# A hybrid attention, state-space and binary-weight kernel: statistics on another engine, identity products at the start, other table and product slots in the scan

## The chip, the cores and the metric

The kernel runs on one core of one Trainium2 chip. The metric is device time in microseconds (us) of one launch, the median of several runs. The core's engines work side by side, each through its own queue in order: TensorE (PE in the profile, its weight loads PEld), VectorE (DVE), ScalarE (ACT), GpSimd (POOL) and SyncE (SP), which here only issues DMAs. An instruction that has to wait holds up everything behind it on its engine.

## The reference

`x` is 4 batches of 1024 rows of 128 channels, float32. Four blocks follow one another, each with a residual sum and a layer norm ahead of it: windowed and strided attention with 16 heads of 8, a three-layer perceptron (MLP) with weights +1 and -1, a selective state-space block (256 inner channels, 16 states), and the MLP again.

```python
x = x + attention(layernorm(x), Wq, Wk, Wv, Wo)
x = x + mlp(layernorm(x), k0, k1, k2, s0, s1, s2)
x = x + mamba(layernorm(x), ln_g, ln_b, W_in, conv_w, ...)   # has its own residual inside
x = x + mlp(layernorm(x), k0, k1, k2, s0, s1, s2)
...
# the recurrence in mamba, for each of 256 channels and 16 states
dA = jnp.exp(dt_t[..., None] * A)
h = dA * h + (dt_t * u_t)[..., None] * B_t[:, None, :]
y_t = jnp.einsum('ben,bn->be', h, C_t)
```

## The kernel before

**Layout.** The batches go in two pairs. `xs[0]` and `xs[1]` hold a pair each: 128 partitions are 64 rows of each of the two batches, and 16 tiles `m` of 128 channels lie along the free dimension. A chunk `c` is 4 such tiles.

**Attention** (line 199) loops over 32 tiles, 16 of each pair, as a pipeline written out by hand: step `i` does the scores of tile `i+1`, the softmax of tile `i`, the strided products of tile `i-1` on GpSimd, their sums on VectorE, and so on to the residual of tile `i-5`. All its instructions are recorded while `keep` holds a value, so each engine runs them in the order in which they are written. The setup computes the first layer norm statistics and turns the weights: `weights_in` (line 232) transposes four weights on TensorE as soon as they are loaded. The residual of a tile `m` under 8 is a VectorE sum, that of a later tile a ScalarE copy from PSUM (`residual`, line 552). For pair 0 the statistics of the MLP behind the attention are taken in the loop too (`mlp_stats`).

**The stage between** (the `while` at line 1390) runs the first pair's MLPs and what the first scan needs. Here `keep` is empty, and a scheduler is free to place the instructions on each engine's queue, also among those of the attention ahead of them.

**The scans** (line 1097) are 128 units: 8 parts (a batch and a half of its 1024 steps; the order is `parts_in_order`), with 16 states `n` each. A unit `i` is:

- GpSimd: `drive(i)` makes `db`, the product of `du` with a row of B (128x1024);
- ScalarE: `decay(i, h)`, for each of the halves `h` of the 256 channels, makes `da = exp(dt * A)` (128x512);
- VectorE: two scans (128x512, `tensor_tensor_scan`) and, for most units, two products with the row of C into `hc`. For the states in `BY_GP` GpSimd makes this product instead, one 128x1024 instruction (`product_by_gp`); the scan then writes to `hs` and not over `da`;
- TensorE: turns `hc` with the identity and sums it over the states in PSUM.

`da` has three buffers in all and `db` three, so a decay can start only when the scan or product that last read its buffer is done. In a part that is the first half of its batch, ScalarE also copies the last column of each half's scan (`carry`).

**The planner.** The rest of the work (the MLPs of both pairs, the norms, what later parts need) is cut into pieces and put between the units by `pieces` (line 1328), by estimated costs of the engines. In each unit it is called twice: once between `decay(i+1, 0)` and `decay(i+1, 1)`, once behind both and behind the sums. A piece that empties PSUM banks is an eviction; one marked `lump` is a *table visit*: two ScalarE activations (Silu for `gate` and `u`, Softplus for `dt`) that need another function table than the exponential of the decays, so a table load stands ahead of them and another behind. A visit may come only where `pieces` is called with `lumps` true. Order on each engine is then kept as recorded.

**Statistics of the MLP behind pair 1's attention** (`stats_ahead(("a", 1, c), ...)`, line 1406) are a stream of such pieces in the scans. `ln_sums` (line 148) takes them there on ScalarE: for each tile an Identity and a Square activation with a sum, and each of these has an accumulator read behind it; four small GpSimd instructions of `ln_stats` and two scalings follow for each chunk. With `soon=True` it takes them on VectorE (`bn_stats`, `bn_aggr`) and needs no scaling.

**The tail.** Behind the last unit the remaining MLP pieces run, then the MLP of the last half.

The core of the loop over the units, from line 1240 on:

```python
product_by_gp(i - 1)
drive(i + 2)
decay(i + 1, 0)
...            # the scans and the VectorE products of unit i
pieces(t + 1.3)
...            # carry copies around decay(i + 1, 1), kept sums
pieces(t + 2.2, lumps=False)
```

Of the kernel before, what the change touches and what calls it, by code (L numbers as in the profile page):

```python
# [26 lines left out]
P = 128  # L27
# [10 lines left out]
E, N, DC, DR = 256, 16, 4, 8  # L38
# [5 lines left out]
def hybrid_kernel(ctx: ExitStack, tc: tile.TileContext, x, Wq, Wk, Wv, Wo, ln_g, ln_b, W_in, conv_w,  # L44
# [17 lines left out]
    ve, te, sc, gp = (InOrder(e) for e in (nc.vector, nc.tensor, nc.scalar, nc.gpsimd))  # L62
# [18 lines left out]
    xs = []  # L81
    for bp in range(NP):
        t = xpool.tile([P, NT, C], F32, tag=f"x{bp}", name=f"x{bp}")
# [11 lines left out]
    ident = const.tile([P, P], F32, name="ident")  # L95
# [103 lines left out]
    def attention(actx):  # L199
# [11 lines left out]
        def spare(name):  # L211
            return pr.tile([P, CH], F32, tag="pr", name=name)
# [16 lines left out]
        load_x(0, range(1, NT // 4), nc.sync)  # L229
        load_x(1, range(NT // 4), nc.sync)  # L230

        def weights_in():
            wt = spare("wt")
            for i in range(4):
                te.transpose(wt[:, i * C : (i + 1) * C], wsrc[:, i], ident)
            sc.copy(wqkv.rearrange("p i c -> p (i c)"), wt[:, : 3 * C])
            sc.copy(woT, wt[:, 3 * C :])


        norms, sums = {}, {}  # L240
# [347 lines left out]
        last = len(tiles)  # L588
# [140 lines left out]
    CT = NT // 4  # L729
# [92 lines left out]
    def stats_ahead(key, needs, tiles_of, soon=False):  # L822
        yield Piece(ready=lambda: all(k in fed for k in needs), same=True)
        known[key] = yield from ln_stats(tiles_of(), "f" + "_".join(map(str, key)), soon)
# [78 lines left out]
    units = [(b, f, n) for b, f in parts_in_order for n in range(N)]  # L903
# [193 lines left out]
    def scans(wide, ready):  # L1097
# [2 lines left out]

        bss, css, dbs, das, hss, hs_of = {}, {}, {}, {}, {}, {}
        BY_GP = (4, 6, 9, 11, 14)
        DIRECT = 1
        sums, kept, py, turned = {}, {}, {}, []
        last = len(units) - 1
# [20 lines left out]
                )  # L1126

        def by_gp(i):
            return units[i][2] in BY_GP and i < last - 1

        def product_by_gp(i):

# [100 lines left out]
        for i, (b, f, n) in enumerate(units):  # L1233
            now[0] = i
            load(i + 3)
            product_by_gp(i - 1)
            drive(i + 2)
            done["db", i + 2] = spend("gp", 2.38, *after(("hs", i - 1, 1)))
            decay(i + 1, 0)
            done["da", i + 1, 0] = spend("sc", 0.69, *after(("hc", i - 1)))  # L1240
            db = dbs.pop(i)
            hss[i] = m2.tile([P, NH, CH], F32, name=f"hc{i}", tag="hc", bufs=5)
            if by_gp(i):
                hs = hs_of[i] = m1.tile([P, NH, CH], F32, name=f"hs{i}", tag="hs", bufs=2)
                hs = [hs[:, h] for h in range(NH)]
            else:
                hs = [das[i, h] for h in range(NH)]
            for h in range(NH):
                first = carry[b % 2][:, h, n : n + 1] if f else 0.0
                ve.tensor_tensor_scan(hs[h], das.pop((i, h)), db[:, h], first, ALU.mult, ALU.add)  # L1250
                done["hs", i, h] = spend("ve", 1.2 if f else 1.14, *after(("da", i, h), ("db", i)))
            if not by_gp(i):
                for h in range(NH):
                    ve.tensor_mul(hss[i][:, h], hs[h], row_of(css, i))
                    done["half", i, h] = spend("ve", 0.6)
                done["hc", i] = times["ve"]
            t = times["ve"]
            pieces(t + 1.3)
            for h in range(NH):
                if f == 0:  # L1260
                    sc.copy(carry[b % 2][:, h, n : n + 1], hs[h][:, CH - 1 :])
                    spend("sc", 0.17, *after(("hs", i, h), ("half", i, h)))
                if h == 0:
                    decay(i + 1, 1)
                    done["da", i + 1, 1] = spend("sc", 0.67, *after(("hs", i, 0), ("half", i, 0)))
            for part in over(i, 1):
                keep_sum(*part)
                done["kept", i] = spend("sc", 0.6, *after(("sum", i - 1)))
            done["sum", i] = spend("pe", total(i), *after(("kept", i)))
            for part in over(i, 0) if i == last else ():  # L1270
                keep_sum(*part)
                turn_sum(*part)
                spend("pe", 0.5, spend("sc", 0.6, times["pe"]))
            t = times["ve"]
            pieces(t + 2.2, lumps=False)
        total(last + 1)
        for h in range(NH):
            gate_by(*units[last][:2], h)
# [3 lines left out]
    times = dict(pe=0.0, ve=0.0, sc=0.0, gp=0.0)  # L1282
# [45 lines left out]
    def pieces(until, lumps=True):  # L1328

        forced = not until
        evictions(lumps, forced)
        for k, rate in RATES.items():
            owed[k] = min(max(owed[k], -2 * rate) + (0 if forced else rate / 2), rate / 2)
        left = SPARE - sum(w.held for w in works)

        for w in works[:-2] + sorted(works[-2:], key=lambda w: w.count):

            moved = w in emptied and now[0] < len(units) - 10  # L1340
            while w.may() and not w.next.evict and w.next.banks <= left:
                if moved and not w.next.same and not (forced and w in emptied):
                    break
                if not (forced or w.next.hurries()):
                    if any(us and owed[k] <= 0 for k, us in w.next.us.items()):
                        break
                    if "pe" in w.next.us and ends(w)[0]["pe"] > until:
                        break
                left -= w.next.banks
                issue(w)  # L1350
                moved = True
            if forced and moved:
                break
# [5 lines left out]
    def stream(*kinds):  # L1359
        for k in kinds:  # L1360
            yield from k
# [5 lines left out]
    def in_scan_buffers(u):  # L1367
# [5 lines left out]
    lanes = [  # L1373
        Work(stream(
            early(0, lane, f1, lane, *[in_scan_buffers] * lane),
            early(0, 2 + lane, f1, lane),
            early(1, lane, f1, lane),
            early(1, 2 + lane, f1, lane),
            *(late(0, 2 * q + lane, f1, lane) for q in range(CT // 2)),
            late_batch(B - 2 + lane, 0, range(4), f1, lane),  # L1380
            late_batch(B - 2, 1, range(2 * lane, 2 * lane + 2), f1, lane),
# [3 lines left out]
    with banks(8):  # L1385
        first = [
            Work(stream(*(mamba_norm(0, c) for c in first_half))),
            Work(mamba_pre_half(*parts_in_order[0])),
        ]
        while (*parts_in_order[0], NH - 1) not in prepared:  # L1390
            wanted = first[-1].may() and "pe" in first[-1].next.us
            for w in first + ([] if wanted else lanes):
                if w.may():
                    w.run()
        for w in lanes:
            while w.next.evict or w.held:
                w.run()
    with banks(SPARE), tc.tile_pool(name="wide", bufs=1, space=PSUM) as wide:
        keep.append(True)
        works.extend([  # L1400
            first[-1],
            Work(stream(*(mamba_pre_half(*k) for k in parts_in_order[1:]))),
            Work(stream(*(mamba_norm(0, c) for c in second_half), *(mamba_norm(1, c) for c in range(CT)))),
            Work(stream(mamba_out(0, 0), mamba_out(0, 1), *(mamba_out_own(*k) for k in parts_in_order[4:-1]))),
            Work(stream(
                *(stats_ahead(("a", 1, c), [], lambda c=c: xs[1][:, 4 * c : 4 * c + 4, :]) for c in range(CT)),
                *(
                    stats_ahead(
                        ("b", 0, c), [("o", b, c // HALF) for b in range(2)],
                        lambda c=c: xs[0][:, 4 * c : 4 * c + 4, :],  # L1410
                    )
                    for c in range(CT)
                ),
                *(
                    stats_ahead(("c", *k), [("o", *k)], lambda k=k: own_x[k], soon=bool(k[1]))
                    for k in parts_in_order[4:-1]
                ),
            )),
            *lanes,
        ])  # L1420
        among_scans[0] = True
        scans(wide, ready)
        among_scans[0] = False
        works.insert(0, Work(mamba_out_own(B - 1, 1)))
        while any(w.next for w in works):
            able = [
                w for w in works if w.may() and (w.next.evict or w.next.banks <= SPARE - sum(v.held for v in works))
            ]
            issue(min(able, key=lambda w: max(ends(w)[0].values(), default=w.since)))
        keep.clear()  # L1430
# [34 lines left out]
```

## Time and profile before

| what | us |
|---|---|
| median of 3 runs | 877.41 (877.21 to 879.07) |
| the profiled execution's own time | 877.82 |
| its span in the profile | 876.0 |
| attention | 0 to about 244 |
| between attention and the first scan | 244 to 318.8 |
| the 128 units of the scans | 318.8 to 832.7 |
| tail | to 876.0 |

The span is what the instructions take from the first to the last; 1.8 us of the profiled execution lie outside it. In a profile's rows `out<-in` names the tiles without their numbers, the bracket at the end gives how long the engine sat idle just before and who ended that wait. Nearly every row has line 57, because one helper there issues all the kernel's instructions: the tile names tell the rows apart.

### The profile page before, as it was taken

How to read it: one execution, taken by the hardware profiler on the slowest of the kernel's cores; microseconds unless marked ns; L12 is line 12 of the kernel's file. 1: busy time of each engine (PE TensorE's matmuls, PEld its weight loads, DVE VectorE, ACT ScalarE, POOL GpSimd, SP SyncE). 2: the span in 40 equal slices, each digit the busy share in tenths (PEclk: the TensorE clock that was granted, in tenths of full speed). 3: DMA queues.
4: the chain of work that ended last, by engine and by line, in shares of the span. 5: the costliest groups of instructions: out<-in, count | busy, mean ns of one | idle time of the engine just before them, and what ended most of it. 6: DMA issues, size and time to landing. Idle time of an engine off the chain costs nothing. (4 is left out here: it accounts for less than half of the span.)

```text
span 876.0 us, 18186 instructions
## 1 busy us (share of the span) xinstructions
PE 728.7 (83%) x7008; PEld 535.0 (61%) x7008; DVE 704.4 (80%) x1037; ACT 603.4 (69%) x1407; POOL 660.2 (75%) x475
## 2 busy tenths in 40 slices
PE   5897778966798979579988888877998978879897
PEld 2454545544677646337757666644866647777777
DVE  6799998999652248788896899797898889999932
ACT  4776657754363569988986599878788976755443
POOL 6699966899332058997898698997988988988600
PEclk9899979999579999687997999887999988999999
DMA  4743133330010043243342234342444343453100
GB/s 129 135 74 74 28 58 70 73 74 2 3 47 1 0 187 108 103 161 125 134 155 100 97 133 149 109 142 100 149 152 147 120 160 121 144 192 139 43 19 19
DMA packets 56438, 87.03 MB, mean 99 GB/s; under 512 B 5800, under 2 KB 39376, under 8 KB 56352
## 3 DMA queue, kind: packets, MB, share of 16 engines
q1 hardware_dynamic: 55248, 85.41, 32.0%
q8 instruction: 55, 0.90, 0.4%
q0 software_dynamic: 544, 0.20, 0.2%
q10 hardware_dynamic: 560, 0.26, 0.1%
q14 instruction: 31, 0.25, 0.1%
HBM read 79.30 MB, written 4.72 MB: 96 GB/s over the span
## 5 line engine op out<-in xcount | busy, mean ns | idle before, releaser
L57 POOL TENSOR_TENSOR db<-du,bs 128x1024 f32<-128x1024 f32 x128 | 301.6, 2374 | 27.4 <-DVE da L57 23.2
L57 ACT ACTIVATE da<-dt,a_t 128x512 f32<-128x512 f32 x256 | 174.5, 687 | 59.6 <-DVE hc L57 49.5
L57 PE MATMUL psT<-ident,hc 128*128 128x128 f32 x1016 | 138.4, 283 | 3.1 <-POOL hc L57 2.9
L57 PEld LDWEIGHTS psT<-ident,hc 128*128 128x128 f32 x1016 | 122.0, 146 | 29.8 <-issue 17.4
L57 DVE TENSOR_TENSOR_SCAN da<-da,db 128x512 f32<-128x512 f32 x88 | 104.3, 1217 | 40.4 <-ACT da L57 20.0
L57 DVE TENSOR_TENSOR_SCAN da<-da,carry,db 128x512 f32<-128x512 f32 x90 | 111.3, 1281 | 5.3 <-ACT da L57 5.3
L57 DVE TENSOR_TENSOR hc<-da,cs 128x512 f32<-128x512 f32 x178 | 113.2, 680 | 0.0
L57 POOL TENSOR_TENSOR hc<-hs,cs 128x1024 f32<-128x1024 f32 x39 | 92.5, 2372 | 22.4 <-issue 9.6
L57 POOL TENSOR_TENSOR prodv<-vS,E 128x128 f32<-128x128 f32 (+14 forms) x30 | 69.4, 2313 | 12.3 <-ACT E L57 12.1
L57 PE MATMUL pga<-h1a,w 128*128 128x512 f32 x256 | 68.5, 419 | 6.8 <-DVE gate L57 3.5
L57 POOL TENSOR_TENSOR prod<-kv,qs 128x128 f32<-128x128 f32 (+14 forms) x30 | 71.0, 2368 | 1.1 <-DVE or L57 1.0
L57 ACT ACT_TABLE_LOAD x48 | 61.6, 1283 | 3.4 <-issue 2.6
L57 PEld LDWEIGHTS pga<-h1a,w 128*128 128x128 f32 x256 | 49.1, 198 | 21.9 <-DVE h1a L57 4.5
L57 PE MATMUL pc<-mxnT,w_conv 128*128 128x512 f32 x128 | 58.4, 593 | 0.9 <-ACT gate L57 0.9
L57 ACT ACTIVATE E<-S 128x512 f32<-128x512 f32 (+15 forms) x62 | 26.5, 473 | 40.1 <-DVE S L57 39.9
L57 DVE TENSOR_TENSOR_SCAN hs<-da,carry,db 128x512 f32<-128x512 f32 x38 | 47.0, 1276 | 7.1 <-ACT da L57 7.1
L57 DVE TENSOR_TENSOR_SCAN hs<-da,db 128x512 f32<-128x512 f32 x40 | 46.9, 1208 | 4.3 <-ACT da L57 4.3
L57 PE MATMUL ps<-kx,qT 64*32 64x256 f32 x1008 | 43.1, 410 | 6.1 <-DVE S L57 5.2
L57 ACT COPY ep<-pt 128x512 f32<-128x512 f32 x32 | 18.7, 586 | 36.7 <-DVE eo L57 36.4
L57 POOL TENSOR_TENSOR du<-dt,u 128x512 f32<-128x512 f32 x16 | 20.3, 1283 | 27.6 <-ACT dt L57 27.6
L57 PE MATMUL pgb<-h1b,w 128*128 128x512 f32 x128 | 35.7, 427 | 4.7 <-DVE x L57 2.4
L57 PEld LDWEIGHTS pc<-mxnT,w_conv 128*128 128x128 f32 x128 | 22.9, 190 | 22.4 <-issue 20.6
(238 smaller groups left out, 1681.0 us busy)
## 6 DMA issues: line engine op xcount, KB each, us to landing
bs<-bd SPq DMA_DIRECT2D x64, 512.0 KB
cs<-bd SPq DMA_DIRECT2D x64, 512.0 KB
vr<-vd SPq DMA_DIRECT2D x32, 256.0 KB
vd<-kv SPq DMA_DIRECT2D x8, 256.0 KB
x<-in_L_attn_a_x_dram SPq DMA_DIRECT2D x15, 128.0 KB
kx<-kT SPq DMA_DIRECT2D x104, 16.0 KB
out_dram<-x SPq DMA_DIRECT2D x8, 128.0 KB
taps<-in_L_attn_b_conv_w_dram SPq DMA_DIRECT2D x1, 512.0 KB
```

The lines of the kernel that those rows point to most:

```text
L57: ins = getattr(self.engine, name)(*args, **kwargs)
```

## The change

There are four edits.

1. **Identity products.** `keep_busy` multiplies the identity with itself on TensorE into a PSUM bank that nobody reads: 5 times ahead of the weight transposes, 8 times behind their copies.
2. **Statistics.** The stream for pair 1's MLP leaves the scans. All of it is issued in the stage between, once the second lane of the MLPs has run 12 pieces, with `soon=True`. In the built program the scheduler has placed it far ahead: the 16 pairs of VectorE instructions stand among the attention's last tiles, one pair for each tile of pair 1 soon after its residual. For the first 11 tiles the `bn_stats` stands between the sum of the strided scores and the row maximum, and the `bn_aggr` between the maximum and the subtraction. GpSimd's four instructions for each of the first three chunks stand between the attention's products or behind the last, those of the fourth ahead of the first norm of the scans' input.
3. **Six late products.** In the last 16 units GpSimd makes the products of states 3, 5, 7, 9, 11 and 13. Before, it made those of 4, 6, 9 and 11 there (14 was left out near the end).
4. **Table visits.** In a unit whose product GpSimd makes, a visit may not come in the first call of `pieces` any more but in the second, behind both decays. In the other units it stays in the first.

```diff
+        def keep_busy(name, times):
+            idle = spare(name)
+            for _ in range(times):
+                te.matmul(idle[:, :P], ident, ident, start=True, stop=True)
+
         def weights_in():
+            keep_busy("idle0", 5)
             wt = spare("wt")
             for i in range(4):
                 te.transpose(wt[:, i * C : (i + 1) * C], wsrc[:, i], ident)
             sc.copy(wqkv.rearrange("p i c -> p (i c)"), wt[:, : 3 * C])
             sc.copy(woT, wt[:, 3 * C :])
+            keep_busy("idle1", 8)
...
         BY_GP = (4, 6, 9, 11, 14)
+        BY_GP_LAST = (3, 5, 7, 9, 11, 13)
...
         def by_gp(i):
-            return units[i][2] in BY_GP and i < last - 1
+            return units[i][2] in (BY_GP if i <= last - N else BY_GP_LAST)
...
-            pieces(t + 1.3)
+            pieces(t + 1.3, lumps=not by_gp(i))
...
-            pieces(t + 2.2, lumps=False)
+            pieces(t + 2.2, lumps=by_gp(i))
...
+        ahead = Work(stream(*(
+            stats_ahead(("a", 1, c), [], lambda c=c: xs[1][:, 4 * c : 4 * c + 4, :], soon=True) for c in range(CT)
+        )))
         while (*parts_in_order[0], NH - 1) not in prepared:
+            while lanes[1].count >= 12 and ahead.next:
+                ahead.run()
...
-                *(stats_ahead(("a", 1, c), [], lambda c=c: xs[1][:, 4 * c : 4 * c + 4, :]) for c in range(CT)),
```

In the built program the planner's other pieces shift with these edits. Behind the first two table visits (units 1 and 2, the same in both) there are 20 more in either kernel. Before, all stood in the first call, 6 of them in units with a GpSimd product: 22, 25, 62, 68, 91 and 94. After, ten stand in the first call of other units (5, 18, 29, 34, 47, 51, 55, 66, 82, 99) and ten in the second call of units with a GpSimd product (9, 14, 22, 25, 43, 57, 78, 86, 91, 94).

## The prediction

> **What bounds the kernel now.** I read the page's busy shares and slices first, then the windows by parts of the scans, the groups of VectorE with what ended their idle time, and the timeline around single places.
>
> ```profile
> PE 728.7 (83%) x7008; PEld 535.0 (61%) x7008; DVE 704.4 (80%) x1037; ACT 603.4 (69%) x1407; POOL 660.2 (75%) x475
> DVE  6799998999652248788896899797898889999932
> POOL 6699966899332058997898698997988988988600
> ```
>
> VectorE is nearly full from slice 3 to 10 (the attention) and from 17 to 37 (the scans), and is the engine to follow in both. The windows of the parts, with the columns PE, PEld, DVE, ACT, POOL:
>
> ```profile
> 318.80:383.30 64.50, 47.67 (x220) 30.90 (x218) 53.36 (x72) 57.90 (x132) 55.07 (x42) 0.84 0.36 128
> 520.10:586.00 65.90, 54.01 (x274) 37.62 (x275) 57.57 (x66) 57.95 (x121) 61.90 (x45) 0.90 0.37 130
> 713.60:771.20 57.60, 50.18 (x306) 40.40 (x305) 56.98 (x66) 37.45 (x74) 52.74 (x30) 0.94 0.44 151
> ```
>
> The seventh part shows what a part costs when VectorE hardly waits (0.6 in all): 57.6. The first six take 63 to 71, and about 9 to 11 of that is VectorE idle. The groups say why:
>
> ```profile
> L57 DVE TENSOR_TENSOR_SCAN da<-da,db 128x512 f32<-128x512 f32 x88 | 104.3, 1217 | 40.4 <-ACT da L57 20.0 <-PE pz L57 12.8 <-POOL db L57 7.1
> L57 DVE TENSOR_TENSOR_SCAN hs<-da,carry,db 128x512 f32<-128x512 f32 x38 | 47.0, 1276 | 7.1 <-ACT da L57 7.1
> ```
>
> With the two scan groups not shown, VectorE's waits among the units are 36.7 for a decay, 7.1 for a GpSimd product, and 13 in its evictions for TensorE: 57. (The 12.8 is the wait ahead of the first unit.) Going through the units, all but 0.2 of the 36.7 follows a table visit. Unit 25, whose product GpSimd makes, ScalarE then VectorE:
>
> ```profile
> 423.03 0.67 ACT L57 ACTIVATE da<-dt,a_t 128x512 f32<-128x512 f32 x1
> 423.72 1.28 ACT L57 ACT_TABLE_LOAD   x1
> 425.01 1.27 ACT L57 ACTIVATE u<-pc,cb 128x512 f32<-128x512 f32 x2
> 426.36 1.28 ACT L57 ACT_TABLE_LOAD   x1
> 427.66 0.69 ACT L57 ACTIVATE da<-dt,a_t 128x512 f32<-128x512 f32 x1
> ...
> 421.60 2.34 DVE L57 TENSOR_TENSOR_SCAN hs<-da,db 128x512 f32<-128x512 f32 x2
> 423.85 1.21 DVE L57 TENSOR_TENSOR_SCAN da<-da,db 128x512 f32<-128x512 f32 x1
> 428.38 1.23 DVE L57 TENSOR_TENSOR_SCAN da<-da,db 128x512 f32<-128x512 f32 x1 [3.32 <-ACT da L57]
> ```
>
> The two decays of unit 26 lie 4 us apart with the visit between; VectorE is through unit 25 in 2.25, does one scan and waits 3.32. The six visits in such units cost 13.5 together (2.24 each), the 14 in other units 23.0 (1.64 each).
>
> **Edit 1, identity products.** The first projection against the same one a chunk later:
>
> ```profile
> 10.97 2.07 PE L57 MATMUL pk<-xnT,wqkv 128*128 128x512 f32 x2 [0.67 <-ACT xnT L57]
> 22.00 1.13 PE L57 MATMUL pk<-xnT,wqkv 128*128 128x512 f32 x2 [1.44 <-ACT xnT L57]
> ```
>
> TensorE is half as fast early on, though the granted clock reads 1.00 in both windows; it is fast once it has worked through 10.97 to 14.6. A 128x128 float32 product is two records; at the slow rate a record is a quarter of 1.04, so 0.52 a product. The 5 take 2.6, from the identity at 1.70 to 4.3: hidden, since the weights land at 4.57. The 8 take 2.8 (0.35 each, as the skip products at the fast rate: 22.2 over 64) to 4.2, from 5.9 to between 8.7 and 10.1. The normed tiles arrive at 8.6 to 9.8, so the cover is just enough; if slow to the end, the chain starts up to 0.9 late. In return the pair of projections (10.97 to 14.6) runs in the 2.0 it takes at 22.00, and the copy of `pq`, the score copies and the next chunk behind them move up; VectorE's `kx` products wait for `pk` alone and gain 1.0. I take **-1.2** (-1.7 to +0.9).
>
> **Edit 2, in the attention.** 11 of the 16 pairs stand where VectorE has no gap over 0.06 us (150 to 229), each inside this triple:
>
> ```profile
> 199.80 1.75 DVE L57 TENSOR_REDUCE S<-prod 128x192 f32<-128x1536 f32 x1
> 201.58 0.90 DVE L57 TENSOR_REDUCE mx<-S 128x16 f32<-128x704 f32 x1
> 202.51 0.89 DVE L57 TENSOR_TENSOR S<-S,mx 128x704 f32<-128x704 f32 x1
> ```
>
> Each of these starts 0.03 after the end of the one it depends on, where an independent instruction starts 0.08 before it. A `bn_stats` and `bn_aggr` in such seams fill two bubbles of 0.11. Interleaved with independent work the pair takes 0.26 (rows at 275.85 to 276.11), so 0.04 is left at best; as a dependent pair it takes 0.40 (4.77 to 5.16). I take 0.15, nearer to the interleaved rows: 11 x 0.15 = **+1.7** (+0.4 to +4.4). The other five fall into waits of 2.65 to 2.91 for `pa` behind 229, or 0.26 beside the weight conversions at 245: nothing. Late tiles' residuals are ScalarE copies that end about 0.9 after `eo`; the sum of 1.9 ahead of the statistic covers that. GpSimd's four instructions (0.23, 1.04, 0.23, 0.20: 1.7) stand twice in its full stretch; its products end 1.6 to 2.3 ahead of VectorE's reads, which hides 1.7 narrowly. If not: up to 3.4.
>
> **Edit 2, in the scans.** ScalarE loses 16 x (0.31 + 0.19) and 16 x (0.40 + 0.19): 17.3 between 320 and 470. It isn't the bound, so by itself this is worth nothing; it lets the MLP pieces come earlier. GpSimd loses 4 x 2.2. One such group (375.23 to 377.44) stands right ahead of the `db` that unit 15 waits 1.66 for. The 3.58 of unit 12 follows five norm instructions and both `du` in a row; after, a `db` stands between the `du`, 1.2 sooner. Together **-2.9** (0 to -7.1).
>
> **Edit 4.** In the second place the visit starts when the unit's second scan is done and the carry copied: 2.35 + 0.16. It lasts 1.30 + 1.27 + 1.30, less overlap 0.12: 3.75. The next decay ends 6.95 into the unit. VectorE wants it at 2.25 + 3.43 (a unit with its own product, as unit 24): 5.68. A wait of 1.3, now at the first scan of unit `i+2`. Without carry copies it starts behind the second decay, at 1.95: 6.4 against 5.92, 0.5. VectorE's evictions in the two units come off. Of the ten: units 9 and 94 have no eviction (2.6), 14 and 78 one of 0.75 (1.1), 22, 25, 86 and 91 at least 1.28 (0), 43 and 57 no carry (1.0): 4.7; I take 6, for other ScalarE work ahead of the decays, which in unit 25 made 0.9. The same arithmetic gives 2.35 for the visit of unit 94 before, measured 2.45. The ten visits left in the first place cost 1.64 each: 16.4. So 36.7 becomes 22.4: **-14.3**. Bounds: 0 to 3.3 (the largest wait) for each moved visit: -20.3 to +12.7.
>
> A rule against this: the Trainium skill, "ScalarE: Activation LUTs", section "What ACT_TABLE_LOAD costs", has a drain of about 1.38 us with every load of 1.28, 2.66 together. By it a visit would take an estimated 6.6, and the moved one would hold VectorE for about 4. The rows above show the next activation 1.29 after a load begins, so I go by the trace.
>
> **What comes next.** As these waits go, GpSimd comes close: 345 of the 394 us of the first six parts, 61.9 of 65.9 in the fourth. Less 8.8 of work in 377 it is at 89%, as VectorE. I give back a third of what was saved: **+5** (0 to +17).
>
> **Edit 3.** A unit given to GpSimd takes 2.37 of VectorE and not 3.55. What follows the last parts:
>
> ```profile
> 813.49 0.71 PE L57 MATMUL pmo_1own<-w_out,gate 128*128 128x128 f32 x4 [2.29 <-DVE ox L57]
> ...
> 834.55 1.14 PE L57 MATMUL pys<-ident,yT 128*128 128x128 f32 x8 [0.24 <-ACT yT L57]
> ```
>
> From 813.49 TensorE has no gap up to 834.3 and few behind it, and it starts on VectorE's eviction `ox` in unit 122. By then GpSimd has four units of the part and not three: -1.2. The sixth product comes behind this and is worth nothing, as TensorE's queue holds the same work. GpSimd needs 3 x 2.37 = 7.1 for a pair of units, VectorE 5.92 and about 1.4 of evictions: it keeps up, without margin. **-1.2** (-2.4 to +3). The skill's "GPSIMD Engine Reference", section "Key points", says GpSimd shares its SBUF interfaces with VectorE and contends with instructions of two SBUF inputs. The rows show none: three `db` at 313.69 with VectorE idle for most of it take 7.02, and the mean of all 128 is 2.374.
>
> **Sum.** -1.2 + 1.7 - 2.9 - 14.3 + 5 - 1.2 = -12.9, against 877.82 of the profiled execution (span 876.0 and 1.8 outside it): 864.9. That execution lies 0.4 above the median, so **864.5**.
>
> **Rivals.**
> - *The wait only moves.* Each moved visit costs in its new place the 2.24 that it did: 22.4 + 16.4 = 38.8, +2.1. With -1.2, +1.7, -2.9, -1.2 that is -1.5: 876. For it: visits wait in ScalarE's queue for other work too. Against it: VectorE has 3.43 of own work behind such a unit, and in the old place 1.2.
> - *Slower: visits ahead of both decays of the next unit starve VectorE.* Place: the first scan of unit `i+2`. At 3.3 each, the largest wait now, 33 + 16.4 is 12.7 more; with -3.6 for the rest, 886.5. It makes the kernel slower from 2.4 a visit ((20.3 + 3.6) / 10). For it: both decays and all evictions now queue behind the visit. Against it: the arithmetic that meets unit 94.
> - *The attention pays in full.* 4.4 and 3.4 in place of 1.7: 870.6. For it: two full engines there. Against it: the seams.
>
> **How the numbers follow.** Forecast 0.57, attention in full 0.17, wait only moves 0.14, slower 0.12. A measurement tells about 0.2% (1.75 us) from no change. The third case straddles that line: half of it counts as faster. Faster 0.81, same 0.07, slower 0.12. The forecast's own range is 857 to 871; with the attention case and the third inside, **856 to 877** leaves out the slower case and a little at the low end.
>
> **What would show it.** Right: `pk` near 1.1 at the start; VectorE's idle time for `da` among the units near 22, now mostly at first scans; the first unit about where it is now (318.8, within 1.5); TensorE gapless behind the `pmo_1own` of the third batch. Wrong: waits of over 2.4 at first scans behind moved visits, waits for `db` over 10 in all, gaps of VectorE between 150 and 229, or a first unit after 322.

## The result

The changed kernel takes 883.83 us (median of 4 runs, 882.74 to 884.62), the kernel before, beside it on the same chip, 878.24 (877.21 to 879.56): a ratio of 1.0077, 95% interval 1.0055 to 1.0099. It is slower by some 6 us where 13 less were forecast. The profiled execution took 882.74, with a span of 880.9.

### The profile page after: what moved, and what is told of

The parts are those of the page before. It is cut to its first block, busy times and chain, and to the rows that moved or that the text cites. A ratio compares the mean times of both kernels' runs of the same rounds, so it can differ in the third digit from the quotient of the medians.

```text
span 880.9 us, 18196 instructions
## 1 busy us (share of the span) xinstructions
PE 732.0 (83%) x7034; PEld 539.6 (61%) x7034; DVE 707.1 (80%) x1065; ACT 592.7 (67%) x1343; POOL 663.1 (75%) x469
## 5 line engine op out<-in xcount | busy, mean ns | idle before, releaser
L57 PE MATMUL psT<-ident,hc 128*128 128x128 f32 x1016 | 140.5, 286 | 2.0 <-POOL hc L57 2.0
L57 DVE TENSOR_TENSOR_SCAN da<-da,db 128x512 f32<-128x512 f32 x88 | 103.6, 1215 | 28.4 <-ACT da L57 12.8
L57 DVE TENSOR_TENSOR_SCAN da<-da,carry,db 128x512 f32<-128x512 f32 x86 | 106.3, 1275 | 16.4 <-ACT da L57 14.4
L57 POOL TENSOR_TENSOR hc<-hs,cs 128x1024 f32<-128x1024 f32 x41 | 97.2, 2370 | 18.8 <-PE psT L57 7.1
L57 DVE TENSOR_TENSOR hc<-da,cs 128x512 f32<-128x512 f32 x174 | 110.3, 676 | 0.1
L57 PE MATMUL pga<-h1a,w 128*128 128x512 f32 x256 | 70.3, 428 | 9.0 <-DVE h1a L57 5.0
L57 POOL TENSOR_TENSOR prodv<-vS,E 128x128 f32<-128x128 f32 (+14 forms) x30 | 69.4, 2314 | 10.1 <-ACT E L57 9.9
L57 ACT ACT_TABLE_LOAD x48 | 61.6, 1283 | 3.5 <-issue 2.6
L57 DVE TENSOR_TENSOR_SCAN hs<-da,carry,db 128x512 f32<-128x512 f32 x42 | 51.7, 1268 | 5.0 <-ACT da L57 5.0
L57 PE MATMUL pgb<-h1b,w 128*128 128x512 f32 x128 | 38.2, 448 | 6.2 <-ACT dt L57 2.6
```

What stands on the lines that cost most here:

```text
L57: ins = getattr(self.engine, name)(*args, **kwargs)
```

## The profile after

The page's busy shares of the changed kernel, and the slices of VectorE and GpSimd:

```profile
PE 732.0 (83%) x7034; PEld 539.6 (61%) x7034; DVE 707.1 (80%) x1065; ACT 592.7 (67%) x1343; POOL 663.1 (75%) x469
...
DVE  6799998999653158778788977898988888999932
...
POOL 6799966899542078877987987898987978889800
```

No engine is notably busier than before: ScalarE lost 10.7 us of work, VectorE has 2.7 more. What grew is idle time, and the slices show where: VectorE reads 7 and 8 from slice 16 to 22 and from 24 to 26, where it had three 9s and a 6 before. The windows of the same three parts as before (columns as there):

```profile
316.89:390.56 73.67, 60.85 (x288) 43.85 (x287) 58.04 (x79) 59.45 (x120) 57.61 (x37) 0.84 0.37 123
519.39:590.26 70.87, 57.22 (x291) 40.74 (x289) 56.89 (x65) 56.74 (x120) 60.35 (x42) 0.88 0.35 120
714.59:777.70 63.11, 52.59 (x332) 42.55 (x332) 58.38 (x66) 40.80 (x81) 51.01 (x28) 0.95 0.39 133
```

The first scan starts at 316.89 and not 318.80, but the first part then takes 73.67 and not 64.50, the fourth 70.87 and not 65.90, the seventh 63.11 and not 57.60. The last part (60.3 against 61.6) gains. The groups of the page name the waits:

```profile
L57 DVE TENSOR_TENSOR_SCAN da<-da,db 128x512 f32<-128x512 f32 x88 | 103.6, 1215 | 28.4 <-ACT da L57 12.8
L57 DVE TENSOR_TENSOR_SCAN da<-da,carry,db 128x512 f32<-128x512 f32 x86 | 106.3, 1275 | 16.4 <-ACT da L57 14.4
...
L57 DVE TENSOR_TENSOR_SCAN hs<-da,carry,db 128x512 f32<-128x512 f32 x42 | 51.7, 1268 | 5.0 <-ACT da L57 5.0
```

Summed over all VectorE instructions among the units, waits are 66.2 us and were 57.3: for a decay 42.2 (36.7 before), for TensorE 16.9 (13.0), for GpSimd 3.0 (7.1), for a carry copy 1.1, unexplained 3.0. That is the sum to carry through the experiments: the units' time less VectorE's waits lies between 453 and 458 us in the profile of every kernel below, so what a kernel loses among the units, it loses as VectorE's waits.

## Experiments: each edit by itself

At this point I held three theories. V: the second place of the visits costs the time. E: pair 1's statistics are ready too early, and its MLPs crowd the first parts. P: the planner, told other things, makes another list of the same pieces, and its quality varies (L, for list, in the later rounds). "Before" is the kernel before, run in the same round (877.28).

Edit 1 alone (the two `keep_busy` calls):

```diff
+            keep_busy("idle0", 5)
...
+            keep_busy("idle1", 8)
```

> The kernel before with the identity products alone. The planner's pieces and all visits stay where they were. All theories: 0.5 to 1.7 us less, as the first projection runs at the fast rate and the first unit of the scans starts that much sooner; the 1.9 us by which the first unit came sooner with all edits would be this edit and nothing else. If the first unit is not sooner by more than 0.5, the 1.9 came from the statistics' edit.

Measured: 874.1 us, ratio 0.9967 (0.9951 to 0.9983): 2.9 us, more than was expected.

Edit 2 alone (the statistics):

```diff
+            while lanes[1].count >= 12 and ahead.next:
+                ahead.run()
...
-                *(stats_ahead(("a", 1, c), [], lambda c=c: xs[1][:, 4 * c : 4 * c + 4, :]) for c in range(CT)),
```

> The kernel before with the statistics' edit alone. The planner moves 18 of its 20 later visits; seven stand in the first call of units with a GpSimd product (6 before). Theory V (the second place of the visits costs the time): about as before or faster, since ScalarE loses 17 us in the scans: 870 to 878. Theory E (pair 1's MLP starts too early and collides with the first parts): slower by 4 to 9, most of it in the first two parts. Theory P (the planner's list of places is reshuffled and the waits fall by chance): any sign, the first part not singled out.

Measured: 875.26, ratio 0.998 (0.9966 to 0.9995). VectorE's waits among the units fall from 57.3 to 54.5; those for GpSimd are gone (7.1 to 0).

Edit 3 alone (six late products):

```diff
+        BY_GP_LAST = (3, 5, 7, 9, 11, 13)
...
+            return units[i][2] in (BY_GP if i <= last - N else BY_GP_LAST)
```

> The kernel before with the six late GpSimd products alone. Visits and pieces ahead of unit 112 stay as they were. The forecast's step: 1.2 us less, by one more unit ahead of the eviction that TensorE's last stretch starts on. Rival: nothing or slower, as the last stretch on TensorE does not start sooner or a product of GpSimd ends late; then the last 16 units are shorter by 2.4 and the tail longer by as much.

Measured: 876.43, ratio 0.9989 (0.9973 to 1.0005). The last part takes 60.5 and not 61.6, the seven before it agree with the kernel before to 0.03 us each.

Edit 4 alone (the visits):

```diff
-            pieces(t + 1.3)
+            pieces(t + 1.3, lumps=not by_gp(i))
...
-            pieces(t + 2.2, lumps=False)
+            pieces(t + 2.2, lumps=by_gp(i))
```

> The kernel before with the table visits' edit alone. Six visits stand in the second call (units 4, 11, 14, 22, 84, 91) and 14 in the first call of other units. Theory V: slower by 3 to 10, with VectorE's idle time behind the six at 2.4 or more each. The forecast's own step: faster by 5 to 9, less than 1 behind each of the six. Theory P: the visits that stay in the first place cost another sum than 1.64 each (before), by more than the six moved ones change.

Measured: 876.85, ratio 0.999 (0.9968 to 1.0012). The time hides what the trace of this run shows. VectorE's waits for a decay fall from 36.7 to 23.9, close to the 22.4 of the forecast, and what VectorE waits in the two units behind a moved visit is 1.6 us (0.7 for a decay, 0.9 for a carry copy). But its waits for TensorE double, from 13.0 to 26.4, and those for carry copies and other work of ScalarE, which were nothing, come to 7.7. All its waits are 60.0 and not 57.3, and the units take 517.2 us and not 514.0. The first scan came 2.9 sooner in this profile, and nothing ahead of the scans is changed by this edit (the last section has how much that start varies).

By the times no edit loses by itself, so V and E, each of which blames one edit, both fall in their plain form: what loses is a combination, or the list that comes with it.

## Experiments: combinations

`e123` is the changed kernel without edit 4, `e24` the kernel before with edits 2 and 4.

```diff
 e123, against the changed kernel:
-            pieces(t + 1.3, lumps=not by_gp(i))
+            pieces(t + 1.3)
...
-            pieces(t + 2.2, lumps=by_gp(i))
+            pieces(t + 2.2, lumps=False)
```

> Identity products, statistics on VectorE and the six late products together; the table visits stay where the kernel before has them. All theories of this round want the same here, since none of the three edits alone lost time: the sum of their single ratios (0.9967, 0.998, 0.9989) is 0.9936, that is 871.6 us against 877.3, between 869 and 875. Above 877 the loss would sit in these three edits together, and neither the visits nor their list would be to blame.

> Statistics and table visits together, without the identity products and the late products. If edits only add up, their single ratios 0.998 and 0.999 give 0.997, 874.7 us. If the loss of the changed kernel is what these two do to each other (the changed kernel's 1.0077 less what identity products and late products bring alone, 0.9967 and 0.9989), 1.0121, some 888 us. Between 880 and 890 says interaction of these two; below 877 says that identity or late products take part.

Measured: e123 873.06, ratio 0.9935 (0.9912 to 0.9958); e24 888.75, ratio 1.013 (1.0108 to 1.0151). The loss sits in edits 2 and 4 together, though neither has one alone, and it is as large as the single ratios leave over. In e24 VectorE's waits, part by part, are those of the changed kernel to 0.1 us up to the seventh part. Both edits feed the planner: edit 2 takes 45 pieces out of its streams (620 before, 575 after), edit 4 tells it other places. So the list became the suspect.

## Experiments: a written list in place of the planner

To part the place of a visit from the list, I replaced the planner by the list that it had made. A digit names one of the eight streams of work and issues its next piece (1 holds the visits, 2 the gate products, 3 the norms, 6 and 7 the MLPs); the strings are the calls, two for each unit, and the tail.

```diff
+    ORDER = (
+        ...
+    ).split(".")
+    calls = iter(ORDER)
+
     def pieces(until, lumps=True):
-        ...
+        for k in next(calls):
+            issue(works[int(k)])
```

With the list as recorded, each engine has the same instructions in the same order. `r_moved` takes e123's list and sets its eight visits at units of GpSimd's product behind both decays, `r_back` takes the changed kernel's list and sets its ten back between them:

```diff
 r_moved, unit 9:             first call   second call
-                             136          136
+                             36           1136
 r_back, unit 14:
-                             6            161376
+                             61           61376
```

> The planner is replaced by a written list of which piece goes where, and the list is that of e123 with one difference: its eight visits at units whose product GpSimd makes (9, 14, 20, 25, 36, 54, 57, 75) stand behind both decays instead of between them. Theory M (the second place itself costs: the visit now stands ahead of both decays of the unit after next): the changed kernel moves ten visits and lies some 12 us above what e123 should have, 1.2 us a visit, so r_moved is about 10 us above e123, 1.011 of it. Theory L (the place costs nothing or gains a little; the planner, told of other places, puts all the pieces in other units, and that list is the worse one): within 3 us of e123, or below it. My forecast's prices (1.64 less for a moved visit, less what GpSimd gives back) would want e123 less 5 to 13.

> The written list of the changed kernel, with its ten visits of the second place put back between the decays of the same units, and all else in its place. Theory M: the loss goes, about 872 us, 0.994 of the kernel before. Theory L: the list is what is bad, so it stays at 880 to 886, 1.003 to 1.010.

Measured: r_moved 868.96, ratio 0.9913 (0.9884 to 0.9941), the fastest kernel of this study, below the kernel before and the changed one. r_back 895.69, ratio 1.0211 (1.0187 to 1.0236). On a fixed list the second place is the better one both times. Against e123 it gains 4.1 us by the medians, but the two intervals overlap, and the units alone differ by 2.6 in the profiles (508.4 and 511.0). Against the changed kernel it gains 11.9, well clear of the noise; r_back lies above what either theory expected. Theory M, a loss from the place, is refuted. And r_moved and the changed kernel hold the same four edits, with visits in the same kinds of places: they are 14.9 us apart by the list alone (waits 52.3 and 66.2).

`r_before_moved` does the same to the kernel before: its own list, six visits moved (units 22, 25, 62, 68, 91, 94).

> The written list of the kernel before, and its six visits at units of GpSimd's product (22, 25, 62, 68, 91, 94) behind both decays: the move of the fourth edit by itself, with nothing else re-planned. From the two pairs so far the move brings 0.5 us a visit (r_moved against e123) or 1.2 (r_back against the changed kernel): 3 to 7 us less than before, 0.992 to 0.997. If e4_visits (0.999) had lost nothing to its new list, the move would be worth 0.1 us a visit, and this run would lie at 0.999 too.

Measured: 875.12, ratio 0.9984 (0.9968 to 1.0): 1.4 us, less than the 3 that I had thought the least, and the interval just reaches no change. The waits for decays near the six visits fall from 13.5 to 0.8, yet VectorE's waits in all only from 57.3 to 53.9. In the kernel before, the second scan of unit 23 waited for its decay:

```profile
415.83 1.23 DVE L57 TENSOR_TENSOR_SCAN da<-da,db 128x512 f32<-128x512 f32 x1 [2.27 <-ACT da L57]
```

The timeline of r_before_moved around unit 22 shows where the gain goes; ScalarE first, then VectorE, then GpSimd:

```profile
409.58 0.69 ACT L57 ACTIVATE da<-dt,a_t 128x512 f32<-128x512 f32 x1
410.60 0.19 ACT L57 COPY carry<-hs 128x1 f32<-128x1 f32 x1 [0.33 <-DVE hs L57]
410.81 1.28 ACT L57 ACT_TABLE_LOAD   x1
...
410.49 2.32 DVE L57 TENSOR_TENSOR_SCAN da<-da,db 128x512 f32<-128x512 f32 x2
412.72 1.26 DVE L57 TENSOR_TENSOR hc<-da,cs 128x512 f32<-128x512 f32 x2
415.30 1.23 DVE L57 TENSOR_TENSOR_SCAN da<-da,db 128x512 f32<-128x512 f32 x1 [1.32 <-POOL hc L57]
417.00 1.23 DVE L57 TENSOR_TENSOR_SCAN da<-da,db 128x512 f32<-128x512 f32 x1 [0.47 <-ACT da L57]
...
412.81 2.40 POOL L57 TENSOR_TENSOR hc<-hs,cs 128x1024 f32<-128x1024 f32 x1
```

Both decays of unit 23 now stand ahead of the table load, and its two scans run as one row without a gap; before, the second waited 2.27. But unit 24 then waits 1.32 for GpSimd's `hc` and 0.47 for a decay. Units 22 to 24 take 11.76 us (before: 2.25 + 5.80 + 3.44 = 11.49): nothing is left. Over the six places, three units each, the time falls by 3.4 us (76.4 to 73.0). What took over, over all units, is the carry copies, which now stand behind the visit (+3.4), GpSimd (+1.3) and TensorE (+0.9).

Next, what makes the changed kernel's list bad. Its longest waits have a common look. VectorE and then TensorE of the changed kernel, at unit 14:

```profile
378.39 2.33 DVE L57 TENSOR_TENSOR_SCAN hs<-da,db 128x512 f32<-128x512 f32 x2
386.47 0.75 DVE L57 SCALAR_TENSOR_TENSOR x<-pfoa,total,x 128x512 f32<-128x512 f32 x1 [5.75 <-PE pfoa L57]
...
375.65 1.13 PE L57 MATMUL pz<-mxnT,w_in 128*128 128x512 f32 x2 [1.46 <-ACT mxnT L57]
377.93 2.07 PE L57 MATMUL pz<-mxnT,w_in 128*128 128x512 f32 x2 [1.15 <-DVE h1a L57]
379.80 1.91 PE L57 MATMUL psT<-ident,hc 128*128 128x128 f32 x8
381.50 4.93 PE L57 MATMUL pfoa<-w,h2a 128*128 128x128 f32 x32
```

An eviction was placed in the same unit as half of the matmuls that it empties. This unit has only two scans on VectorE, so VectorE is there 5.75 us before TensorE, which had itself waited twice just before. At unit 47 ScalarE walks into the same trap inside a visit:

```profile
516.90 1.28 ACT L57 ACT_TABLE_LOAD   x1
518.72 0.69 ACT L57 ACTIVATE u<-pc,cb 128x512 f32<-128x512 f32 x1 [0.54 <-PE pc L57]
523.03 0.69 ACT L57 ACTIVATE u<-pc,cb 128x512 f32<-128x512 f32 x1 [3.62 <-PE pc L57]
523.74 1.28 ACT L57 ACT_TABLE_LOAD   x1
...
525.76 1.29 DVE L57 TENSOR_TENSOR_SCAN da<-da,carry,db 128x512 f32<-128x512 f32 x1 [5.08 <-ACT da L57]
```

The row would read as a wait for a decay; the visit ahead of it stood still for 4.16 us, for the matmuls of `pc`. `r_fix` sets five such pieces later in the changed kernel's list, four by a call or two and the visit of unit 47 behind both decays; with pieces that stood beside them it is 13 in all (unchanged calls are left out):

```diff
 unit                         first call   second call
-12                           6337         371
+12                           637          3371
-14                           6            161376
+14                           6            117
-15                           7
+15                           6763
-47                           1135576      71
+47                                        113557671
-52                           2            23
+52                           2            3
-53                           1337         37
+53                           21337        37
-78                           65           1157
+78                           5            1157
-79                           7556
+79                           67556
```

> The written list of the changed kernel with five pieces set one call later, those at which VectorE waits longest: TensorE's product pfoa is taken up in unit 15 and not in 14 (wait 5.75 us), the visit at unit 47 stands behind both decays (5.08), the second gate product in unit 53 and not in 52 (3.67), pfob in unit 79 and not in 78 (3.30), the mxn pieces of unit 12 behind both decays (3.36). Together 21.2 us of VectorE's waits. Theory C (the changed kernel's loss is made of a few such collisions, each of which costs its wait): at least half comes back, 870 to 876, 0.992 to 0.998 of the kernel before. Theory T (TensorE is simply late in those parts, and VectorE's wait only shows it): the waits turn up at the next piece, 881 to 885.

Measured: 873.91, ratio 0.9958 (0.9937 to 0.9979), 9.9 us below the changed kernel; waits fall from 66.2 to 56.1. TensorE and VectorE of r_fix at the same place:

```profile
378.08 2.33 PE L57 MATMUL pz<-mxnT,w_in 128*128 128x512 f32 x4 [1.47 <-ACT mxnT L57]
380.25 1.03 PE L57 MATMUL psT<-ident,hc 128*128 128x128 f32 x8
381.12 3.74 PE L57 MATMUL pfoa<-w,h2a 128*128 128x128 f32 x32
...
379.75 2.33 DVE L57 TENSOR_TENSOR_SCAN hs<-da,db 128x512 f32<-128x512 f32 x2
381.99 2.32 DVE L57 TENSOR_TENSOR_SCAN da<-da,db 128x512 f32<-128x512 f32 x2
384.22 1.26 DVE L57 TENSOR_TENSOR hc<-da,cs 128x512 f32<-128x512 f32 x2
385.40 0.74 DVE L57 SCALAR_TENSOR_TENSOR x<-pfoa,total,x 128x512 f32<-128x512 f32 x1
```

The eviction comes behind unit 15 and waits for nothing. The other four: 5.08 became 1.99 (now for `h1a`), 3.67 became 0.6, 3.30 became 1.32, and the 3.36 of unit 12 stayed (3.40). The time lies in theory C's range and far from T's, so the loss was for the most part made of a few collisions. Of the 21.2 us of waits 10.1 are gone in all, a little under the half that C expected, and new waits of 1.27 and 1.35 for a decay stand in units 49 and 80: a part does turn up again, as T had it.

## Experiments: other lists by chance

Is a list planned with edit 4 worse by rule, or did this one come out badly? Eight more lists answer, from the same pieces: the planner stays, and one of its constants is changed by 4 to 5%.

```diff
 p_e123, p_after, p_before, p_e4:
-    RATES = {"pe": 3.3, "ve": 1.2, "sc": 2.4, "gp": 1.2}
+    RATES = {"pe": 3.3, "ve": 1.2, "sc": 2.3, "gp": 1.2}
 p2_e123, p2_after:
+    RATES = {"pe": 3.3, "ve": 1.2, "sc": 2.5, "gp": 1.2}
 p3_e123, p3_after:
-            pieces(t + 2.2, ...
+            pieces(t + 2.3, ...
```

> e123 with one price of the planner changed by 4% (ScalarE's share per call 2.4 to 2.3), which gives another list of the same pieces with the visits in the first place. Theory L-chance (the lists differ in luck, several us either way): anything from 868 to 885. Theory L-rule (a list planned with the fourth edit is worse by rule): within 4 us of e123, 869 to 877, and p_after stays above 879.

> The changed kernel with the same price of the planner changed (2.4 to 2.3): another list, with ten visits in the second place. L-chance: anything from 866 to 885, so as likely below the kernel before as above it. L-rule: 879 to 888.

> e123 (without the fourth edit) with ScalarE's share per call at 2.5 and not 2.4. L-chance: anything from 868 to 885. L-rule: 869 to 877.

> The changed kernel with ScalarE's share per call at 2.5 and not 2.4; the list is the same up to about unit 50, so the wait of 5.75 us for pfoa in unit 14 and that behind the visit at unit 47 should still be there. L-chance: 870 to 888. L-rule: 879 to 888.

> e123 (without the fourth edit) with the horizon of the planner's second call at 2.3 and not 2.2. L-chance: anything from 868 to 885. L-rule: 869 to 877.

> The changed kernel with the horizon of the planner's second call at 2.3 and not 2.2; the list is the same in its first half, with the same two waits. L-chance: 870 to 888. L-rule: 879 to 888.

> The kernel before with ScalarE's share per call at 2.3 and not 2.4: another list, all visits in the first place. L-chance: anything from 870 to 890. L-rule: within 4 us of the kernel before, and below p_e4.

> The kernel before with the fourth edit and ScalarE's share per call at 2.3: ten visits in the second place, on a list that shares nothing with the changed kernel's. L-chance: anything from 870 to 890, as likely below p_before as above it. L-rule: at least 4 us above p_before.

Measured, with the lists that the planner makes unchanged beside them:

| visits as in the kernel before | ratio | with edit 4 | ratio |
|---|---|---|---|
| kernel before | 1 | e4_visits | 0.999 (0.9968 to 1.0012) |
| p_before | 1.0219 (1.0195 to 1.0243) | p_e4 | 1.0002 (0.9984 to 1.002) |
| e123 | 0.9935 (0.9912 to 0.9958) | changed kernel | 1.0077 (1.0055 to 1.0099) |
| p_e123 | 1.0088 (1.0066 to 1.0111) | p_after | 1.0001 (0.9985 to 1.0018) |
| p2_e123 | 0.9965 (0.9948 to 0.9982) | p2_after | 1.0059 (1.0027 to 1.0092) |
| p3_e123 | 0.9975 (0.9954 to 0.9996) | p3_after | 1.0106 (1.0078 to 1.0135) |

One constant off by 4% moves the kernel before by 19.7 us (896.2 against 876.55), e123 by 10.9 and the changed kernel by 7.1 the other way. The two columns overlap, and their means are 1.003 and 1.004.

Within the rows of edits 1 to 3 the right column is higher three times in four, but p3_after shares nearly the whole first half of its list with the changed kernel and p2_after all but two calls of the first 15 units, and both keep the wait of 5.76 in unit 14 and one of over 5 in unit 48, so they are hardly new draws (p2_e123 and p3_e123 are no full ones either: their first two parts take as long as those of e123 to 0.6 us); on the other base, edit 4 came out better with the changed constant.

Theory L-rule is contradicted by p_e123 (883.92), p_after (876.76) and p_e4 (877.03); p_before, at 896.2, lies above what either theory expected. A rule against edit 4 isn't shown, though a small tendency can't be excluded with so few lists. Chance of several us either way is shown.

## Why the prediction was wrong

**Edit 1** (-1.2): right in kind. The first projection of `pk` in the changed kernel:

```profile
10.96 1.13 PE L57 MATMUL pk<-xnT,wqkv 128*128 128x512 f32 x2 [0.68 <-ACT xnT L57]
20.33 1.12 PE L57 MATMUL pk<-xnT,wqkv 128*128 128x512 f32 x2 [1.45 <-ACT xnT L57]
```

It takes 1.13 where it took 2.07, as forecast. One profile can't give the size of the term (the last section says why), but the twenty together can. VectorE's first row maximum (`mx`) starts at 21.79 to 22.45 in the twelve kernels with the identity products and at 22.90 to 23.58 in the eight without: 1.1 sooner in the mean, where 1.2 was forecast. By the ratio of e1_identity the edit brings 2.9 us (1.5 to 4.3); what is above 1.1 stays open. The clock of 1.00 that the prediction read for the slow stretch was no measured one: the trace's first entry for the granted clock stands at 14.33 in the kernel before, behind most of the slow projections, and at 8.53 in the changed kernel, ahead of them.

**Edit 2** (+1.7 in the attention, -2.9 in the scans): the waits for GpSimd, mostly for `db`, went in e2_stats, all 7.1 of them, but of VectorE's waits in all 2.8 were gained, where 2.9 was forecast. The term in the attention can be measured as well, from the row maximum of pair 1's tile 4 to that of its tile 15, a stretch with eleven `bn_stats` and ten `bn_aggr` after the edit. The kernel before, and then the changed kernel:

```profile
152.44 0.76 DVE L57 TENSOR_REDUCE mx<-S 128x16 f32<-128x576 f32 x1
224.02 0.94 DVE L57 TENSOR_REDUCE mx<-S 128x16 f32<-128x752 f32 x1
```

```profile
151.06 0.76 DVE L57 TENSOR_REDUCE mx<-S 128x16 f32<-128x576 f32 x1
224.33 0.93 DVE L57 TENSOR_REDUCE mx<-S 128x16 f32<-128x752 f32 x1
```

The stretch took 71.58 and now takes 73.27; it is 73.1 to 73.3 in the thirteen profiles with this edit and 71.4 to 72.0 in the seven without. That is 1.5 us in the mean, so the term was right. The only gap of VectorE of any size between 150 and 229 is 0.64, a wait for GpSimd, so the attention didn't pay in full.

**Edit 3** (-1.2): the last part gained 1.1 to 1.3, and TensorE runs from the third `pmo_1own` batch at 819.13 to 838.13 with no idle time shown. But in e3_late the tail grew by 0.7 (43.2 to 43.9), and the ratio of 0.9989 (0.9973 to 1.0005) isn't clear of no change.

Edits 1 to 3 together were to bring 3.6 us; e123 shows 5.7 (0.9935 of 877.39; 4.3 by the medians).

**Edit 4** is where it failed, in the step "ten visits left in the first place cost 1.64 each: 16.4. So 36.7 becomes 22.4: -14.3". Three things in it, and in the step on what comes next, were wrong.

- The smaller: the step's mechanism is right, its worth was not. On an unchanged list the wait for decays behind a moved visit falls further than I had it, from 2.25 to 0.13 each in r_before_moved (I had 0.6), and in all from 36.7 to 27.3. But 6.0 of these 9.4 us (9.4 less the 3.4 by which all waits fell) come back as other waits of VectorE, where "what comes next" gave back a third.
- A term that was put at nothing: VectorE's waits for TensorE were taken to stay at 13.0, and "what comes next" looked at GpSimd alone. They rose to 16.9 in the changed kernel and to 26.4 in e4_visits, where they took back by themselves all that the decays had given (12.8), while the waits for GpSimd fell from 7.1 to 3.0 and 1.5.
- The larger: prices of one list were used for another. I took the planner's new places from the built program and carried the old mean price over, as if a price belonged to a visit. The ten left in the first place cost 2.46 each in the changed kernel (24.6 in all, not 16.4), the ten moved 0.82 (8.2, where 6 were forecast), and 9.4 stand in units more than two behind a visit, where before there were 0.2: together the 42.2. r_moved has what the forecast meant, all four edits at 868.96, within the range of the forecast's own case. That is in part luck: the move brought 2 to 4 us there, not the 9.3 that the forecast had for it (-14.3 and +5), and the rest is the good list of e123.

Of the rivals, "slower" had the right sign and the wrong cause: it wanted 2.4 us at each moved visit, and the moved visits cost 0.82, or 1.1 with the waits for a carry copy or a `db` behind them. "The wait only moves" is nearest for the edit by itself, as r_before_moved shows, though the wait moves to other engines and not to the next scan. A rival that blames the planner's list was missing, though the places in front of me showed that 20 visits had been dealt anew.

The planner could not warn either. Its own clock for VectorE, which adds up its prices, stands at 538.7 us behind the last unit for e123's list and at 538.6 for the changed kernel's; the chip took 511.0 and 521.1.

## What to carry to other kernels

Where a greedy planner deals out the work, an edit to its inputs is two changes: what it does, and a new draw of the list. Measure the spread of the draw first, by turning a constant that should not matter, and test the edit on a written list, where a moved instruction is all that moves. Look at the longest waits one by one: five collisions taken apart, with 13 pieces set later, gave back more than the whole change had lost.

## What the runs showed of the hardware

**The clock is part of a collision.** The windows around unit 14 of the changed kernel, and then those of r_fix; the first column after the comma is TensorE's busy time, the third from the end its granted clock:

```profile
374.00:378.00 4.00, 1.38 (x5) 0.37 (x3) 3.13 (x5) 3.94 (x11) 4.00 (x2) 0.90 0.34 131
378.00:384.00 6.00, 6.00 (x22) 4.86 (x23) 2.72 (x3) 4.73 (x9) 5.95 (x4) 0.50 0.47 176
```

```profile
376.00:380.00 4.00, 2.46 (x10) 1.11 (x9) 3.64 (x6) 3.97 (x10) 4.00 (x3) 1.00 0.43 131
380.00:386.00 6.00, 6.00 (x51) 5.70 (x50) 6.00 (x7) 5.71 (x10) 6.00 (x4) 1.00 0.47 176
```

In the changed kernel TensorE worked for 1.38 of 4 us and then ran at 0.50 for the next 6, so the 32 matmuls of `pfoa` took 4.93; in r_fix it worked for 2.46 of 4, kept 1.00, and they took 3.74. The Trainium skill's "TensorE: Matmul & The Clock Gate", "Part 1: The HAM clock gate", says that the clock falls to half after an idle window of about 3.4 us. The changed kernel's trace has the clock at half from 377.17 to 383.99, 6.83 us, and each of its other stretches of half clock, but for the one that the end cuts off, also lasts 3.41 us or a whole multiple of it, which fits such a window. But TensorE needn't be idle throughout: here it was busy for a third of the 4 us. So the gaps on TensorE cost twice here: once as gaps, and once in the matmuls behind them.

Beside r_fix, whose four `pz` matmuls take 2.33 together, the half clock cost about 0.9 in the later two (2.07 against 1.13 for the first two), 0.9 in `psT` (1.91 against 1.03) and 1.2 in `pfoa`: 3 of the 5.75 us that VectorE waited. r_fix moved the eviction and a piece of unit 12 at once, and the second gap is gone in it too, so no run shows what the eviction's move alone would have saved.

**The same order repeats to hundredths.** Unit 14 took 8.74, 8.74, 8.76, 8.76 and 8.76 us in the profiles of the changed kernel, e24, p_after, p2_after and p3_after, whose lists agree from unit 11 to there, with the dip of the clock each time. The start does not repeat so well: with the same instructions ahead of it the first scan began between 315.89 and 320.46 in six profiles (the kernel before, e3_late, e4_visits, r_before_moved, p_before, p_e4). A term of 1 or 2 us in the attention can't be read from one profile.
